# Cross attention's probabilities turned in 32x32 blocks by VectorE, and four tiles' values multiplied together on 32x32 tiles of TensorE

## Chip, cores and metric

The kernel runs on one core of one Trainium2 chip. The metric is device time in microseconds, the median of several runs. Below, PE is TensorE, PEld its weight loads, DVE is VectorE, ACT is ScalarE, POOL is GpSimd and SP is SyncE, whose queue issues nearly all DMAs.

## Reference

An encoder layer over a context of 77 tokens and a decoder layer over 2048 tokens, for two batches, in float32, with width 512, 16 heads of 32 and a feed forward of width 2048. What matters here is the decoder's cross attention, whose keys and values come from the encoder's 77 rows:

```python
memory = encoder(ctx)                                   # (2, 77, 512)
y = tgt                                                 # (2, 2048, 512)
y = y + mha(ln(y), ln(y), self weights, causal + relative bias)
y = y + mha(ln(y), memory, cross weights, relative bias)
h = ln(y)
y = y + relu(h @ ff1.T + b1) @ ff2.T + b2

def mha(xq, xkv, ...):
    q, k, v = projections of xq, xkv, xkv               # split into 16 heads of 32
    attn = softmax(q k^T / sqrt(32) + bias)
    return (attn v, heads joined) @ w_out.T + b_out
```

## The kernel before, in words

The whole schedule is written by hand: each engine executes its instructions in the order in which the program issues them. In a first part (to about 1650 us) the encoder and the decoder's self attention run. The second part does cross attention and feed forward. It is cut into 8 *blocks* of 512 tokens (2 batches of 4), and each block into four *tiles* of 128 tokens.

For each block the feed forward takes 56 *slots* (`per`). In slots 0 to 27 `first_product` (L1638) multiplies one weight tile by the block's activations, eight matmul instructions of 256 columns; the matrix products use Strassen's seven products in Winograd's form, so there are sums and differences of quarters in all places. Results go to `hT`, added by VectorE (L1651) or copied by ScalarE (L1648), and then go through ScalarE's relu (L1654). In slots 28 to 55 `second_product` (L1667) takes seven weight tiles in each four slots (2, 2, 2, 1), eight instructions of 128 columns a tile. `sums_h` (half sums L1587; others L1605, L962) prepares its left operands four slots ahead, on VectorE and GpSimd. After each four slots the sums in PSUM are mixed (L1675 to L1683) and added to `y` by GpSimd (L1687).

A float32 matmul is recorded as two instructions (two passes), a transpose as one.

`cross(x)` plans the cross attention of block x into the slots of block x - 1: each of the 56 entries of `plan` is a list of functions, run ahead of the slot's feed forward work. Only blocks 1 to 7 go through it (the first block's cross attention is `first_cross`, done within the first part with the same `attend_stages`). For each tile t of the block, with `at = 13 + 5 t`:

- slot `at`: scores. 16 matmuls (L836), one per head, of 32 partitions each, into four PSUM banks; VectorE takes the maximum (L845) and subtracts it (L846), after adding a bias (L843) for the first two tiles of a batch. The probabilities lie in `pr`, 128 queries x 16 heads x 77 keys.
- `at + 2`: exponential on ScalarE (L849).
- `at + 3`: sums (L854), reciprocals (L855) on VectorE, then GpSimd multiplies (L860).
- `at + 7`: `turned`. 16 TensorE transposes of 128x77 (L866), four to a bank, and four ScalarE copies (L867) to `pts`.
- `at + 11`: `times_v`. 16 matmuls (L874), one per head, values of 77x32 as the stationary operand and 128 queries moving, on four column strips of the array; ScalarE copies the result (L878), and for each second tile `sums_o` makes the sums S1 to S4 (L1785 to L1788).

`o_product` (L1801, result added by L1805) multiplies the output weights in slots 31 to 34 for tiles 0 and 1 and in 40 to 43 for tiles 2 and 3; `norm_stages` for the feed forward's norm (statistics L793 to L797, centring L803, transposes L811 and copies L814) starts in slots 35, 36, 44 and 45. The query projections (`q_product`, L1758) are in slots 9 to 12. Cross attention's PSUM banks are 0 to 3, taken in turn by `bank()`; the feed forward's are 4 to 7.

Weights come in tiles of 256 KB. `feed` (L1541 to L1550) issues their DMAs into a ring of 16 places in the lower half of `pp`, after each slot's products; a place is filled again as soon as PE has read it. `next_w` hands them out in order. Loads of y for a later block (`new_y`, L1361) are issued in slots 28 to 31, stores of the result (L1695) in slots 54 and 2, all from SP's queue.

Of the kernel before, what the change touches and what calls it, by code (L numbers as in the profile page):

```python
# [54 lines left out]
def tile_encoder_decoder(ctx: ExitStack, tc: tile.TileContext, ins, out):  # L55
# [103 lines left out]
    with (  # L159
# [664 lines left out]
        def attend_stages(q, kTc, v, y, biased, pr, pts, place, w_o, bi=None):  # L824


            prh = pr.rearrange("p (h k) -> p h k", k=S)
            by_r = pr.rearrange("p (g r k) -> p g r k", r=HC, k=S)
            keep = {}

            def score():
# [7 lines left out]
                for r in range(HC):  # L839
                    s = banks[r][:, : NC * S].rearrange("p (g k) -> p g k", k=S)  # L840
                    d = by_r[:, :, r, :]
                    if biased:
                        nc.vector.tensor_tensor(d, s, bi[r] if bi else d, ALU.add)  # L843
                        s = d
                    nc.vector.tensor_reduce(mx[:, :, r], s, AX.X, ALU.max)  # L845
                    nc.vector.tensor_tensor(d, s, mx[:, :, r, None].to_broadcast([P, NC, S]), ALU.subtract)  # L846

            def exp():
                nc.scalar.activation(pr, pr, AF.Exp)  # L849
# [496 lines left out]
        prs = [oflat[:, : H * S], pts_all[:, 5:8, :].rearrange("p a k -> p (a k)")[:, : H * S]]  # L1346
        kTc = pts_all[:, 4, : NC * S].rearrange("p (c k) -> p c k", k=S)
        n2_sums, o_sums, vc, qT = [high[:, (4 + k) * D : (5 + k) * D] for k in range(4)], [], [], []
# [21 lines left out]
        def last_loads():  # L1370
            t = sb.tile([P, MB], F32, name="q", tag="q", bufs=3)
            nc.sync.dma_start(t[:S, :], cv_d[:, 0, :])
            vc.append(t)
            xt_ring.append(sb.tile([P, MB], F32, name="q", tag="q", bufs=3))
# [10 lines left out]
        xt_ring, row_ca = [], []  # L1385
# [126 lines left out]
        O_SLOTS = {at + k: js for at in (31, 40) for k, js in enumerate(((0, 1), (2, 3), (4, 5), (6,)))}  # L1512
# [25 lines left out]
        w_ring = [low[:, ts(j, D)] for j in range(16)]  # L1538
        tiles, fed, used = weight_tiles(), [0], [0]

        def feed(upto):  # L1541
            while fed[0] < upto:
# [3 lines left out]
                dst = w_ring[fed[0] % len(w_ring)]  # L1546
# [5 lines left out]
        def next_w(c):  # L1552
            used[0] += 1
            assert used[0] <= fed[0]
            return w_ring[(used[0] - 1) % len(w_ring)].rearrange("p (c o) -> p c o", c=c)
# [14 lines left out]
        mixed = oflat[:, H * S : H * S + 12 * P].rearrange("p (k n) -> p k n", n=P)  # L1570
# [133 lines left out]
        def ff_slot(s):  # L1704
# [11 lines left out]
            feed(used[0] + len(w_ring))  # L1716
# [10 lines left out]
        def cross(x):  # L1727
# [4 lines left out]
            def place(tag):  # L1732
                if tag == "xr":
                    return lambda: sb.tile([P, D], F32, name=tag, tag=tag, bufs=2)
                return next_xt

            for t in range(TB):
                fs = norm_stages(
                    lambda t=t: y_of(x, t), "n2", row_ca[0], place("xt"), lambda t=t: nT2[:, :, ts(t, P)]
# [34 lines left out]

            def of_o(t, name):
                if name[0] == "S":
                    i = int(name[1]) - 1
                    return o_sums[i // 2][:, ts(i % 2, TOK)]
                r, c = int(name[0]) - 1, int(name[1]) - 1
                return held["o", t + r]["oT"][:, ts(c, TOK)]  # L1780

            def sums_o(t):
                s = {n: of_o(t, n) for n in ("S1", "S2", "S3", "S4", "11", "12", "21")}
                a21, a22 = (held["o", t + 1]["bank"][:, ts(c, TOK)] for c in range(2))
                minus(ve, s["S3"], s["11"], a21)  # L1785
                minus(ve, s["S2"], a22, s["S3"])
                ve.tensor_tensor(s["S1"], s["21"], a22, ALU.add)
                minus(gp, s["S4"], s["12"], s["S2"])  # L1788
# [20 lines left out]
            for n, js in O_SLOTS.items():  # L1809
                t = 0 if n < 36 else 2  # L1810
                plan[n].append(lambda t=t, js=js: [o_product(t, j) for j in js])
            bias_1 = None
            if m == 0:

                def next_batch():
                    nc.sync.dma_start(kTc, ckT_d[:, :, ts(b, S)])
                    nc.sync.dma_start(vc[0][:S, :], cv_d[:, b, :])
# [3 lines left out]
                spare = [y_of(x + 1, r) for r in range(HC)]  # L1821
                bias_1 = [a[:, : NC * S].rearrange("p (g k) -> p g k", k=S) for a in spare]
                plan[3].append(lambda: bias_tile(prs[0].rearrange("p (h k) -> p h k", k=S), 2, P, S, 255))
                plan[5].append(lambda: [bias_tile(a, 2, P, S, 255 - P, r, HC) for r, a in enumerate(bias_1)])
            for t in range(TB):
                at = 13 + 5 * t
# [3 lines left out]
                    lambda g, t=t: qT[g // 2][:, g % 2, ts(t, P)], kTc, vc[0][:S, :], y, biased, prs[t % 2],  # L1830
                    lambda g: pts_all[:S, g, :], place("xr"), wbt,
                    bias_1 if biased and t else None,
                )
                held["o", t] = fs[7]
                if t % 2:
                    fs = fs[:5] + (lambda t=t, f=fs[5]: [f(), sums_o(t - 1)],)

                for k, f in zip((0, 2, 3, 3, 7, 11), fs):
                    plan[at + k].append(f)
                fs = norm_stages(y, "n3", bo, place("xt"), lambda t=t: nTt[:, :, ts(t, P)])  # L1840
                at = (35, 36, 44, 45)[t]
# [152 lines left out]
```

## Time and profile before

| | |
|---|---|
| median of 3 runs | 2729.82 us (2728.53 to 2731.02) |
| span of the profiled execution | 2726.8 us |
| PE busy | 2708.1 us (99%) |
| VectorE, ScalarE, GpSimd busy | 1839.9, 1537.0, 1002.4 us |
| one block of the second part (2078 to 2215 us) | 137.0 us |

The profiled execution has its span only, from its first to its last instruction; its time as the runs count it is not listed. Busy times are unions of the instructions' durations, so a pipelined matmul counts until its end. In a group's line the columns are the line of the code, the engine, the operation, output and inputs with shapes, the count, busy time and mean ns of one, and the idle time of the engine just before them with what ended it. In a timeline's line they are start, length, engine, line, operation and count.

### The profile page before, as it was taken

Reading aid. Unit: us, or ns where it says so; the run is one execution under the profiler, and the core shown is the slowest. Engines: PE = TensorE matmul, PEld = TensorE weight load, DVE = VectorE, ACT = ScalarE, POOL = GpSimd, SP = SyncE. Lnnn points to the kernel's source line nnn. Section 1 sums busy time; section 2 is a strip of 40 time slices with the busy share of each in tenths; the row PEclk is TensorE's granted clock in tenths of the full one; section 3 lists DMA queues with packets and bytes.
Section 4 is the critical chain, followed back from the end, with each engine's and each line's share of the span. In section 5 each row is a group of like instructions: output and inputs, shape, how many; then the busy total and the mean of one; then the engine's idle time right before and its main releaser. Section 6 shows DMA issues by size and latency. Waiting matters only on the chain.

```text
span 2726.8 us, 68267 instructions
## 1 busy us (share of the span) xinstructions
PE 2708.1 (99%) x26606; PEld 2217.9 (81%) x26606; DVE 1839.9 (67%) x5445; ACT 1537.0 (56%) x2978; POOL 1002.4 (37%) x844
## 2 busy tenths in 40 slices
PE   9999999999999999999999999999999999999998
PEld 6678877777876677777777777898989898989898
DVE  4776688888885677788888783646464746464645
ACT  3554567777786547667777784444444444444431
POOL 2612235500300513322300203455556565656456
PEclk9999999999999999999999999999999999999999
DMA  8724355511213522343311206565657565656465
GB/s 242 213 92 135 126 155 164 168 50 43 67 45 89 143 76 72 111 133 98 126 50 35 79 19 220 171 214 173 213 171 239 168 216 170 218 166 219 151 224 185
DMA packets 296277, 385.10 MB, mean 141 GB/s; under 512 B 41184, under 2 KB 165648, under 8 KB 295826
## 3 DMA queue, kind: packets, MB, share of 16 engines
q1 hardware_dynamic: 295954, 380.73, 44.1%
q8 instruction: 211, 3.46, 0.5%
q14 instruction: 112, 0.92, 0.1%
HBM read 334.15 MB, written 46.47 MB: 140 GB/s over the span
## 4 chain that ended last, share of the span: by engine, by line
PE 95%; DVE 1%; ACT 1%; DMA 1%; POOL 1%; issue 1%; SPq 0%; DVEq 0%; POOLq 0%; ACTq 0%
PE psum L427 18%; PE psum L1638 14%; PE psum L1667 13%; PE psum L375 11%; PE psum L456 9%; PE psum L1134 8%; PE psum L1801 3%; PE psum L1758 3%; PE psum L1049 3%; PE psum L866 2%; PE psum L836 1%; PE psum L874 1%; PE psum L590 1%; PE psum L811 1%; PE psum L239 1%; PE psum L215 1%
## 5 line engine op out<-in xcount | busy, mean ns | idle before, releaser
L406 ACT ACTIVATE pp<-pp,nm 128x128 f32<-128x128 f32 (+15 forms) x512 | 611.8, 1200 | 28.6 <-DVE nm L401 27.8
L384 DVE TENSOR_SCALAR_CACHE_REDUCE pp<-psum 128x512 f32<-128x512 f32 (+3 forms) x1024 | 556.2, 591 | 51.3 <-PE psum L375 49.7
L434 ACT COPY pts<-psum 128x512 f32<-128x512 f32 x714 | 384.1, 594 | 312.6 <-PE psum L427 265.6
L427 PE MATMUL psum<-ident,pp 128*128 128x128 f32 x4352 | 530.4, 277 | 4.7 <-ACT nT L310 4.0
L427 PEld LDWEIGHTS psum<-ident,pp 128*128 128x128 f32 x4352 | 474.0, 141 | 55.7 <-DVE pp L384 21.4
L375 PE MATMUL psum<-kT,q 32*128 32x512 f32 (+3 forms) x2560 | 336.5, 559 | 2.5 <-DVE q L217 1.0
L456 PEld LDWEIGHTS psum<-pts,vv 128*32 128x32 f32 x8704 | 226.4, 110 | 127.4 <-DVE pp L384 55.4
L1667 PE MATMUL psum<-pp 128*128 128x128 f32 x2560 | 304.5, 276 | 1.9 <-POOL pp L962 1.6
L1667 PEld LDWEIGHTS psum<-pp 128*128 128x128 f32 x2560 | 296.3, 192 | 8.6 <-issue 2.8
L432 DVE COPY pts<-psum 128x512 f32<-128x512 f32 x374 | 245.2, 685 | 82.6 <-PE psum L427 80.3
L456 PE MATMUL psum<-pts,vv 128*32 128x128 f32 x8704 | 279.6, 276 | 0.8 <-DVE mx L391 0.3
L962 POOL TENSOR_TENSOR pp<-pp 128x512 f32<-128x512 f32 x159 | 212.8, 1356 | 111.0 <-DMA pp<-in_dec_ff_wT_dram 50.6
L1638 PE MATMUL psum<-vv,pp 128*128 128x256 f32 x1024 | 236.2, 381 | 0.0
L375 PEld LDWEIGHTS psum<-kT,q 32*128 32x128 f32 x2560 | 146.3, 183 | 107.1 <-issue 41.3
L1638 PEld LDWEIGHTS psum<-vv,pp 128*128 128x128 f32 x1024 | 190.3, 190 | 25.8 <-issue 0.5
L391 DVE CUSTOM_DVE_ANT_0 pp<-psum,bias 128x256 f32<-128x256 f32 (+1 forms) x512 | 196.0, 411 | 19.7 <-PE psum L375 19.7
L1651 DVE TENSOR_TENSOR kT<-kT,psum 128x512 f32<-128x512 f32 x96 | 65.8, 686 | 191.6 <-PE psum L1638 191.4
L1654 ACT ACTIVATE kT<-kT,vecs 128x256 f32<-128x256 f32 x192 | 86.9, 501 | 156.6 <-DVE kT L1651 155.9
L1638 PE MATMUL psum<-nT,pp 128*128 128x256 f32 x768 | 174.1, 380 | 0.5 <-DVE oT L471 0.5
L1638 PEld LDWEIGHTS psum<-nT,pp 128*128 128x128 f32 x768 | 144.2, 190 | 20.8 <-issue 1.4
L1675 ACT COPY oT<-psum 128x128 f32<-128x128 f32 x56 | 15.0, 268 | 238.9 <-PE psum L1667 238.9
L494 POOL TENSOR_TENSOR oT<-rirows,oT 128x512 f32<-128x512 f32 x30 | 38.4, 1280 | 293.6 <-DMA rirows<-rec 181.7
(272 smaller groups left out, 4110.6 us busy)
## 6 DMA issues: line engine op xcount, KB each, us to landing
pp<-w_d SPq DMA_DIRECT2D x520, 256.0 KB
pp<-in_dec_ff_wT_dram SPq DMA_DIRECT2D x112, 256.0 KB
bias<-tzg SPq DMA_DIRECT2D x128, 128.0 KB
pp<-wo_d SPq DMA_DIRECT2D x56, 256.0 KB
wqk<-in_dec_sa_in_wT_dram SPq DMA_DIRECT2D x52, 256.0 KB
wqk<-sa_q SPq DMA_DIRECT2D x84, 128.0 KB
vv<-in_enc_ff_wT_dram SPq DMA_DIRECT2D x8, 1024.0 KB
xr<-in_x_dram SPq DMA_DIRECT2D x32, 256.0 KB
```

The source lines that it names most:

```text
L375: nc.tensor.matmul(banks[r][:, : kn * P], q[rows4(r), ts(t, P)], kT[rows4(r), g, k0 * P : (k0 + kn) * P], start=True, stop=True,)
L384: nc.vector.tensor_scalar(p[:, k0 : k0 + far], s[:, :far], 1.0, None, ALU.mult, ALU.max, accum_out=st["mx"][:, r, c : c + 1],)
L391: nc.vector.tensor_tensor_reduce(p[:, k0 + far : i + 1], s[:, far:kn], near[:, 2 - (kn - far) :], 1.0, LOWEST, ALU.add, ALU.max, accum_out ...
L406: nc.scalar.activation(p, p, AF.Exp, bias=nm, accum_out=to)
L427: nc.tensor.transpose(pt[:, ts(x, P)], state[n]["p"][r][:, k], ident)
L432: nc.vector.tensor_copy(pts[:, : len(load), :], pt[:, :w])
L434: nc.scalar.copy(pts[:, : len(load), :], pt[:, :w])
L456: nc.tensor.matmul(ot[rows4(r)], vv[:, k, ts(g * HC + r, HD)], got.pop((n, k, r)), start=k == k0 and (whole or not begun), stop=k == k1 - ...
L962: engine.tensor_tensor(out, a, b, ALU.subtract)
L1134: nc.tensor.matmul(mm[:, ts(f, TOK)], left[:, c, ts(f, P)], right[:, c, :], start=c == 0, stop=c == 1,)
L1638: nc.tensor.matmul(mm[:, ts(f, TOK)], a[:, c, ts(f, P)], b[:, c, :], start=fresh and f == 0 and c == 0, stop=c == 1, skip_group_check=True,)
L1667: nc.tensor.matmul(psum[:, bank_i, ts(col, P)], lhs[:, c, :], w[:, c, :], start=fresh and k in (0, 3) and c == 0, stop=c == 3, skip_group_ ...
```

## The change

1. The probabilities of all four tiles of a block are kept (`prs`, in the lower half of `pp`, which was the weight ring), each head with 96 places of which 77 are used. VectorE turns a whole tile's probabilities, 128x1536, in 32x32 blocks in place, by one instruction (`blocks_turned`), six slots after the tile's scores. PE's transposes and ScalarE's copies of them are gone.
2. The values are loaded in three pieces of 32 keys, four times, one for each quarter of the partitions (`load_v`, 12 DMAs; the last piece is filled up with zeros). `times_v(g)` multiplies four heads for all four tiles of the block: 3 pieces x 4 quarters x 4 heads = 48 matmuls of 32x32 weights and 128 columns (4 tiles x 32 queries), where the quarter sets the row strip and the PSUM bank and the head the column strip. The four lots are in slots 32 to 35.
3. `values_out` in slot 35 reads the four banks: ScalarE copies to rows for each tile, VectorE and GpSimd make the sums for both pairs of tiles.
4. Scores start in slots 13, 17, 21 and 25, output products in 37 and 41, norms in 41, 42, 45 and 46.
5. The weight ring has ten places: four that remain in `pp` and six of `oT`; the first 22 weight tiles still use the old places.

```diff
+        def heads_of(pr):
+            return pr.rearrange("p (h k) -> p h k", h=H)[:, :, :S]
...
             def exp():
-                nc.scalar.activation(pr, pr, AF.Exp)
+                nc.scalar.activation(prh, prh, AF.Exp)
...
-        prs = [oflat[:, : H * S], pts_all[:, 5:8, :].rearrange("p a k -> p (a k)")[:, : H * S]]
+        KC = 3
+        prs = low[:, : TB * H * KC * RB].rearrange("p (a x) -> p a x", a=TB)
+        v4 = pts_all[:, :KC, :]
...
-        O_SLOTS = {at + k: js for at in (31, 40) for k, js in enumerate(((0, 1), (2, 3), (4, 5), (6,)))}
+        SCORE_AT = (13, 17, 21, 25)
+        VALUES_AT = 32
+        OUT_AT = (37, 41)
+        NORM_AT = (41, 42, 45, 46)
+        O_SLOTS = {at + k: js for at in OUT_AT for k, js in enumerate(((0, 1), (2, 3), (4, 5), (6,)))}
...
-        w_ring = [low[:, ts(j, D)] for j in range(16)]
+        w_places = [low[:, ts(j, D)] for j in (*range(16), *range(6, 12))]
+        w_ring = [low[:, ts(j, D)] for j in range(12, 16)] + [oT_all[:, j, :] for j in range(6)]
...
-        def feed(upto):
-            while fed[0] < upto:
+        def feed(upto=None):
+            while upto is None or fed[0] < upto:
+                dst, before = w_place(fed[0])
+                if before is not None and before >= used[0]:
+                    return
...
+            def load_v(batch):
+                for a in range(P // RB):
+                    for c in range(KC):
+                        n = min(RB, S - c * RB)
+                        nc.sync.dma_start(v4[a * RB : a * RB + n, c, :], cv_d[c * RB : c * RB + n, batch, :])
...
+            def blocks_turned(t):
+                nc.vector.transpose(prs[:, t], prs[:, t])
+
+            def times_v(g):
+                if g == 0:
+                    for _ in range(P // RB):
+                        bank()
+                pT = prs.rearrange("p t (h c q) -> p t h c q", h=H, c=KC)
+                for c in range(KC):
+                    for a in range(P // RB):
+                        for r in range(HC):
+                            h = g * HC + r
+                            nc.tensor.matmul(
+                                psum[rows4(r), a, ts(g, P)], v4[ts(a, RB), c, ts(h, HD)],
+                                pT[ts(a, RB), :, h, c, :], start=(c == 0), stop=(c == KC - 1),
+                            )
...
+            def values_out():
+                got = psum[:, : P // RB, :].rearrange("p a (g t q) -> p t g a q", g=NC, t=TB)
+                for t in range(TB):
+                    g0 = 2 * (t % 2)
+                    nc.scalar.copy(split(o_rows[t])[:, g0:], got[:, t, g0:])
+                for t in (0, 2):
+                    f = {n: split(of_o(t, n)) for n in ("S1", "S2", "S3", "11", "22")}
+                    a21, a22 = (got[:, t + 1, 2 * c : 2 * c + 2] for c in range(2))
+                    minus(ve, f["S3"], f["11"], a21)
+                    minus(ve, f["S2"], a22, f["S3"])
+                    ve.tensor_tensor(f["S1"], a21, f["22"], ALU.add)
+                    minus(gp, of_o(t, "S4"), of_o(t, "12"), of_o(t, "S2"))
...
+            for g in range(NC):
+                plan[VALUES_AT + g].append(lambda g=g: times_v(g))
+            plan[VALUES_AT + NC - 1].append(values_out)
             for t in range(TB):
-                at = 13 + 5 * t
+                at = SCORE_AT[t]
...
-                for k, f in zip((0, 2, 3, 3, 7, 11), fs):
+                fs = fs[:4] + (lambda t=t: blocks_turned(t),)
+                for k, f in zip((0, 2, 3, 3, 6), fs):
                     plan[at + k].append(f)
-                fs = norm_stages(y, "n3", bo, place("xt"), lambda t=t: nTt[:, :, ts(t, P)])
-                at = (35, 36, 44, 45)[t]
+                fs = norm_stages(y, "n3", bo, next_xt, lambda t=t: nTt[:, :, ts(t, P)])
+                at = NORM_AT[t]
```

80 lines of the change are left out of this document (38 added, 42 removed).

## Prediction

> **What bounds the kernel.** I read the page first, for the share of each engine and the chain that ended last.
>
> ```profile
> span 2726.8 us, 68267 instructions
> PE 2708.1 (99%) x26606; PEld 2217.9 (81%) x26606; DVE 1839.9 (67%) x5445; ACT 1537.0 (56%) x2978; POOL 1002.4 (37%) x844
> PE 95%; DVE 1%; ACT 1%; DMA 1%; POOL 1%; issue 1%; SPq 0%; DVEq 0%; POOLq 0%; ACTq 0%
> ```
>
> TensorE (PE) is the bound. The edit lies in the second part of the program, where one block's feed forward runs in 56 slots and the next block's cross attention is spread between them. The windows of one such block, and the chain of waits from 1700 to 2560 us, say how tight that part is.
>
> ```profile
> core 0: us, PE busy (x) PEld busy (x) DVE busy (x) ACT busy (x) POOL busy (x), PEclk, DMA share, GB/s
> 2078.00:2215.00 137.00, 136.98 (x1080) 124.25 (x1079) 80.15 (x157) 57.73 (x123) 78.47 (x67) 1.00 0.65 204
> by line: PE psum L1638 37.6%; PE psum L1667 31.1%; PE psum L1758 8.6%; PE psum L1801 8.4%; PE psum L866 5.4%; PE psum L836 3.3%; PE psum L874 2.9%; PE psum L811 2.6%; issue 0.0%
> ```
>
> A block takes 137.0 us, PE is busy for 136.98 of them at full clock, and every piece of the chain is a PE line. What leaves PE there leaves the time, until another engine is late. Seven blocks carry cross attention in this form (28 tiles); the first block's is done elsewhere and keeps its form.
>
> **What PE loses.** Per tile of 128 tokens, 16 transposes (L866) and 16 value products (L874, two instructions each) go.
>
> ```profile
> L866 PE MATMUL psum<-ident,oT 128*77 128x128 f32 x224 | 28.1, 274 | 0.0
> L866 PE MATMUL psum<-ident,pts 128*77 128x128 f32 x224 | 26.7, 273 | 0.0
> L874 PE MATMUL psum<-pts,q 77*32 77x128 f32 x896 | 30.3, 276 | 0.0
> 2137.40 1.99 PE L1638 MATMUL psum<-vv,pp 128*128 128x256 f32 x8
> 2139.32 1.08 PE L874 MATMUL psum<-pts,q 77*32 77x128 f32 x32
> 2140.33 1.99 PE L1638 MATMUL psum<-nT,pp 128*128 128x256 f32 x8
> 2142.16 1.91 PE L866 MATMUL psum<-ident,pts 128*77 128x128 f32 x16
> 2143.91 1.89 PE L1638 MATMUL psum<-nT,pp 128*128 128x256 f32 x8
> 2145.64 3.62 PE L1638 MATMUL psum<-vv,pp 128*128 128x256 f32 x16
> ```
>
> The transposes are busy for 54.8 us in 28 groups, 1.96 each; the timeline shows that 0.16 of a group lies over the next line (1.91 long, but the next line starts after 1.75). So 1.80 goes per tile. Eight L1638 take 2145.64 - 2143.91 = 1.73 undisturbed, 1.92 before the L874 group and 1.83 after it: entering and leaving small tiles costs 0.19 + 0.10, of which 0.10 at the first belongs to the score group ahead of it, so 0.19 in all. With the group's own 1.01 that is 1.20. Per block 4 x (1.80 + 1.20) = 12.0 us go.
>
> **What PE gains.** Four lots of 48 value products, 96 instructions each, on 32x32 tiles, in slots 32 to 35. No such tile is in the trace. A round of 128 columns takes 1.75 / 16 = 0.109. The 32 instructions of the L874 group need 8 rounds, 0.87 of its 1.01, so four column strips work abreast; the rest and the two changes of mode are 0.33. The score products (L836) show the same for four row strips, each into a bank of its own, as the lots write theirs.
>
> ```profile
> 2149.18 1.13 PE L836 MATMUL psum<-pts,bias 32*128 32x77 f32 x32
> 2150.24 2.05 PE L1667 MATMUL psum<-pp,kT 128*128 128x128 f32 x16
> 126.81 0.74 PE L645 MATMUL psum<-pp 77*32 77x77 f32 x32
> 127.48 1.33 PE L637 MATMUL psum<-ident,pp 77*77 77x77 f32 x16
> ```
>
> The two ends: sixteen abreast is 6 rounds, 0.65 + 0.33 = 0.98 a lot; four abreast is 24 rounds, 2.62 + 0.33 = 2.95. I take 0.98, because strips by columns and strips by rows are each shown four abreast and use different inputs and outputs. Four lots: 3.9 us per block. PE's own balance is -12.0 + 3.9 = -8.1 us per block, -57 us in all.
>
> The Trainium skill, "TensorE: Matmul & The Clock Gate", Part 1, gives a floor of about 25 ns from one matmul's start to the next however small it is; a lot would by it take an estimated 2.4 + 0.33 = 2.7 us and seven blocks 34 us more than now, with the wait below. The L645 group denies it in that form: 32 instructions in 0.67 us are 21 ns each.
>
> **What VectorE (DVE) gains, and who waits.** This is where most of the 57 us go back. One new instruction per tile turns 128x1536 in 32x32 blocks.
>
> ```profile
> L484 DVE STREAM_TRANSPOSE rt<-ri 128x32 f32<-128x32 f32 x30 | 6.3, 212 | 1.0
> L795 DVE TENSOR_SCALAR crs<-cmv 128x1 f32<-128x1 f32 x64 | 9.8, 153 | 2.2
> L854 DVE TENSOR_REDUCE csu<-pts 128x16 f32<-128x1232 f32 x14 | 20.0, 1432 | 23.4 <-ACT pts L849 23.4
> L855 DVE RECIPROCAL cri<-csu 128x16 f32<-128x16 f32 x32 | 8.1, 253 | 1.1
> L1587 DVE TENSOR_TENSOR pp<-kT 128x512 f32<-128x512 f32 x32 | 23.8, 766 | 0.0
> L1605 DVE TENSOR_TENSOR pp<-kT 128x512 f32<-128x512 f32 x24 | 21.2, 883 | 0.0
> L1651 DVE TENSOR_TENSOR kT<-kT,psum 128x512 f32<-128x512 f32 x96 | 65.8, 686 | 191.6 <-PE psum L1638 191.4
> L1676 DVE TENSOR_TENSOR oT<-psum,oT 128x256 f32<-128x256 f32 x56 | 23.3, 417 | 40.2 <-ACT oT L1675 40.2
> 2137.48 0.48 DVE L845 TENSOR_REDUCE cmx<-psum 128x4 f32<-128x308 f32 x1 [0.28 <-PE psum L836]
> 2141.16 0.68 DVE L1651 TENSOR_TENSOR kT<-kT,psum 128x512 f32<-128x512 f32 x1
> 2194.70 7.31 PE L1667 MATMUL psum<-pp 128*128 128x128 f32 x64
> ```
>
> Its price: L854 reads 1232 columns in 1.43, 1.16 ns a column, so 1536 are 1.78 us. The far end comes from the transpose of 32 columns: less a one-column instruction (L795) it has 59 ns for 32, 1.84 ns a column, so 0.15 + 2.83 = 3.0 us. The gap of 32 columns is too small to tell a start-up from a rate; I take 1.78 and keep 3.0 for the range. "VectorE: DVE Perf Modes" of the Trainium skill, in its part on the transpose paths, gives 311 ns for 128 bf16 columns; with the 212 above that is an estimated 1.03 ns a column and 1.76 us, though no run here shows that size.
>
> The lots need all four tiles turned, and DVE works in order. I compare both engines from the third tile's scores (slot 21) to the first lot (slot 32). Nothing of cross attention is left for PE in between but two score groups.
>
> PE: 2 scores at 1.06 + 0.19 (from 2149.18 to 2150.24, and the mode), 7 first products at 1.73, and the 7 weight tiles of slots 28 to 31 at 0.89 each (8 instructions of the 64 that ran through from 2194.70): 2.5 + 12.1 + 6.3 = 20.9 us.
>
> DVE, in its queue: 2 x 8 score reductions and subtractions at 3.7 a set (2137.48 to 2141.16), 7.4; the turns of tiles 1, 2 and 3, 5.3; sums and reciprocals of tiles 2 and 3, 3.4; four L1651 of slots 22 to 25, 2.7; two L1605, 1.8; four L1587, 3.1; one L1676, 0.4. Together 24.1, and it can't begin before the first score group is done, 1.3 later. That ends at 25.4, 4.5 us after PE stands at the lot. In the same chain the exponential of the last tile makes DVE wait a little: L854 idled for 23.4 us in 14 times before, 1.7 each, and I keep 0.7 of it, since DVE now arrives later. So PE waits 5.2 us ahead of the first lot in each block, with its own product of slot 32 and all later ones queued behind. DVE had slack here before because PE still had transposes and value products between.
>
> After the last lot (slot 35) the four banks must be read out before slot 37's first output product: a ScalarE (ACT) copy of 0.6, then six VectorE operations of 0.42 (as L1676), some 3.3 us with the handovers, while PE has 3 weight tiles, 2.7. I put 0.7 there.
>
> **What costs nothing.** ACT loses 16 copies a block (L867, rows below) and gains no more than four; it had 79 idle us in the block's window. POOL's normalisation keeps its length, and its row shows what it waits for: VectorE. The loads of values in twelve pieces come twice in the program, in slots 1 and 10, behind which the weight loads wait; a full ring covers those slots, where a tile lasts 1.73. The ring of ten instead of sixteen leaves nine tiles, 9 x 0.89 = 8.0 us, from a place's release to its next use.
>
> ```profile
> L867 ACT COPY pts<-psum 77x512 f32<-77x512 f32 x112 | 57.1, 586 | 20.4 <-PE psum L866 20.4
> L860 POOL TENSOR_TENSOR pts<-pts,cri 128x1232 f32<-128x1232 f32 x14 | 31.5, 2251 | 59.0 <-DVE cri L855 59.0
> 2193.80:2213.80 20.00, 20.00 (x178) 19.90 (x178) 10.36 (x23) 5.33 (x13) 12.48 (x12) 1.00 0.83 268
> pp<-w_d SPq DMA_DIRECT2D x520, 256.0 KB
> vv<-y SPq DMA_DIRECT2D x24, 256.0 KB
> ```
>
> At 0.83 of the DMA engines' time they moved 268 GB/s, so about 323 at most. Slots 28 to 31 will want 7 tiles and 4 loads of y, 2.9 MB or 8.9 us, in 6.3 us of PE's time; the 2.6 us of arrears lie within the 8.0, and the wait at slot 32 lets the queue catch up.
>
> **The sum.** Per block -12.0 + 3.9 + 5.2 + 0.7 = -2.2 us; seven blocks, -15 us. The span would be 2711.6. The median of the runs, 2729.8, is 3.0 above the span, and I leave that as it is: 2714.6, say 2715. Time from run to run differs by 2.5 us, so 0.2% (5.5 us) is about what a measurement can tell from no change.
>
> **Rivals.**
> - *The lots run slower, and the kernel is slower.* The place is PE in slots 32 to 35. The decisive point is 2.2 / 4 above my price: a lot of 1.5 us, 12 ns an instruction. The fastest group of the trace, L645, took 21 ns with its tail and about 17 without; if that is a limit of issue, a lot is 96 x 0.0166 + 0.33 = 1.9 and the total 2715 + 7 x 4 x 0.92 = 2741. Four abreast makes 2715 + 7 x 4 x 1.97 = 2770. For it: nothing in the trace is issued faster. Against it: L645's rounds of 77 columns (0.066) explain its pace without such a limit. Chance 0.22, with 0.04 of it within 0.2%.
> - *The turn takes 3.0 us.* Three in the stretch add 3.7 to the wait: 2715 + 7 x 3.7 = 2741. For it: the 212 ns. Against it: the other rows' rate. Chance 0.10.
> - *The ring starves PE*, because loads of y and weights collide in the shorter slots 28 to 31: 2 us a block give 2729. For it: 8.9 us of transfers in 6.3. Against it: PE waits anyway just behind. Chance 0.08, 0.05 within 0.2%.
> - *No wait at the first lot*, if VectorE keeps up: 2715 - 36 = 2679. Against it: the two sums above. Chance 0.05.
>
> **The numbers.** My forecast has 0.55, of which 0.03 is within 0.2%. Faster 0.52 + 0.05 = 0.57; same 0.03 + 0.04 + 0.05 = 0.12; slower 0.18 + 0.10 + 0.03 = 0.31. The range 2699 to 2752 leaves out the case without a wait and the slower half of the first rival, about 0.16; it covers a wait at slot 32 between 3 and 8 us and a turn between 1.78 and 3.0.
>
> **What would show it.** L866 and L874 of the seven blocks are gone from PE's groups; the new product's line has 96 instructions in about 0.8 us of each lot. The transpose of 128x1536 has a mean near 1.78. PE's waits show the new product waiting for VectorE's turn, seven times about 5 us, and little else; VectorE is busy almost throughout slots 21 to 31. A lot of over 1.5 us, a turn of over 2.3, or PE waiting for a DMA would prove me wrong.

## The result, and the profile after

The changed kernel takes 2769.25 us, the median of four runs (2766.32 to 2774.15); the kernel before took 2730.1 beside it. The ratio is 1.0148, with a 95% interval of 1.0134 to 1.0163: slower by 1.5%, where 2715 us, and so faster, was forecast. The profiled execution took 2766.32 us, its span is 2764.5, 37.7 more than before. First the page of the changed kernel, with the busy time of the engines and the shares of the chain that ended last.

```profile
PE 2685.6 (97%) x27950; PEld 2192.0 (79%) x27950; DVE 1906.8 (69%) x5473; ACT 1474.9 (53%) x2866; POOL 997.9 (36%) x845
PE 83%; DVE 10%; ACT 3%; issue 2%; POOL 1%; DMA 1%; SPq 0%; DVEq 0%; ACTq 0%; POOLq 0%
```

TensorE is busy for 22.5 us less than before, in a longer span, and VectorE's share of the chain has gone from 1% to 10%. PE executes 1344 matmul instructions more. Next the windows of one block of feed forward with its cross attention (columns as in the prediction), then four stretches around the first lot of that block.

```profile
1961.30:2103.60 142.30, 134.25 (x1274) 120.92 (x1273) 85.64 (x153) 48.89 (x108) 77.16 (x67) 0.98 0.60 181
2018.00:2024.00 6.00, 6.00 (x55) 5.85 (x53) 5.43 (x7) 3.64 (x8) 1.23 (x1) 1.00 0.74 211
2024.00:2027.00 3.00, 0.04 (x1) 0.00 (x0) 3.00 (x4) 0.00 (x0) 2.38 (x2) 1.00 0.97 354
2027.10:2033.80 6.70, 3.95 (x104) 3.39 (x105) 6.67 (x7) 0.00 (x0) 6.18 (x5) 0.50 0.35 132
2033.90:2045.00 11.10, 10.65 (x336) 8.87 (x336) 1.64 (x4) 1.00 (x3) 4.08 (x3) 1.00 0.52 145
```

The block takes 142.3 us instead of 137.0, and PE is idle for 8 of them. At 2024.0 PE stops, 3 us later its granted clock falls to 0.50 and stays there for 6.8 us, the first lot and the next products with it. In six of the seven blocks the clock record has a stretch of half clock of 6.83 us at this place, in one of 10.24. Before, there was none in the blocks. The lengthening of the seven blocks (4.3, 5.2, 5.3, 8.6, 5.1, 4.1 and 5.2 us) adds up to the whole 37.8.

The groups of the new instructions and PE's waits in the second part (engine, line, what it waited for: us in all, times, longest) say who was late.

```profile
L1815 PE MATMUL psum<-pp,pts 32*32 32x128 f32 x2688 | 47.9, 315 | 43.2 <-DVE pp L1804 42.7 <-issue 0.4
L1804 DVE STREAM_TRANSPOSE pp<-pp 128x1536 f32<-128x1536 f32 x28 | 49.5, 1769 | 0.0
PE psum L1815 <- DVE pp L1804: 42.7, 7, 7.9
PE psum L1854 <- DVE pts L1833: 9.1, 7, 1.3
PE psum L1854 <- DVE vv L1858: 3.4, 7, 0.5
```

The turn costs 1.77 us, as forecast. The first lot waits for the last turn for 6.1 us a block. The output products (L1854) wait 1.3 us for the values to leave the banks (L1833), and 0.5 for the result of an earlier output product to be added (L1858). No wait is for a DMA. The timeline of the same block shows PE, then VectorE's queue in the same stretch.

```profile
2022.99 1.06 PE L1687 MATMUL psum<-pp,kT 128*128 128x128 f32 x8
2029.85 2.17 PE L1815 MATMUL psum<-pp,pts 32*32 32x128 f32 x96 [5.81 <-DVE pp L1804]
2031.95 2.95 PE L1687 MATMUL psum<-oT,pp 128*128 128x128 f32 x16
...
2018.59 1.77 DVE L1804 STREAM_TRANSPOSE pp<-pp 128x1536 f32<-128x1536 f32 x1
2020.90 1.44 DVE L857 TENSOR_REDUCE csu<-pp 128x16 f32<-128x1232 f32 x1 [0.54 <-ACT pp L852]
2022.37 0.25 DVE L858 RECIPROCAL cri<-csu 128x16 f32<-128x16 f32 x1
2022.54 3.89 DVE L1607 TENSOR_TENSOR pp<-kT 128x512 f32<-128x512 f32 x3
2026.36 0.41 DVE L1696 TENSOR_TENSOR pts<-psum,pts 128x256 f32<-128x256 f32 x1
2026.69 1.41 DVE L1607 TENSOR_TENSOR pp<-kT 128x512 f32<-128x512 f32 x1
2028.03 1.76 DVE L1804 STREAM_TRANSPOSE pp<-pp 128x1536 f32<-128x1536 f32 x1
```

VectorE has one idle moment, 0.54 us for the exponential of the last tile; from there 8.9 us of its queue lie ahead of the end of the last turn, at 2029.8. PE has 3.2 us of work left at that moment. The two products behind the lot, 16 instructions, take 2.95 us at half clock; behind a lot at full clock they take 2.05, as the second experiment shows.

### The profile page after: what moved, and what is told of

Same layout as the page of the kernel before. It is cut to its first block, busy times and chain, and to the rows that moved or that the text cites. A ratio compares the mean times of both kernels' runs of the same rounds, so it can differ in the third digit from the quotient of the medians.

```text
span 2764.5 us, 70789 instructions
## 1 busy us (share of the span) xinstructions
PE 2685.6 (97%) x27950; PEld 2192.0 (79%) x27950; DVE 1906.8 (69%) x5473; ACT 1474.9 (53%) x2866; POOL 997.9 (36%) x845
## 4 chain that ended last, share of the span: by engine, by line
PE 83%; DVE 10%; ACT 3%; issue 2%; POOL 1%; DMA 1%; SPq 0%; DVEq 0%; ACTq 0%; POOLq 0%
PE psum L427 18%; PE psum L375 11%; PE psum L1687 10%; PE psum L1658 9%; PE psum L456 9%; PE psum L1137 8%; PE psum L1773 3%; PE psum L1854 3%; PE psum L1052 2%; PE psum L1815 2%; DVE pp L849 1%; DVE cmx L848 1%; DVE csu L857 1%; PE psum L590 1%; PE psum L811 1%
## 5 line engine op out<-in xcount | busy, mean ns | idle before, releaser
L965 POOL TENSOR_TENSOR pp<-pp 128x512 f32<-128x512 f32 x159 | 206.8, 1321 | 107.4 <-DMA pp<-in_dec_ff_wT_dram 50.9
L1687 PE MATMUL psum<-oT,pp 128*128 128x128 f32 x1544 | 193.6, 280 | 0.4 <-POOL pp L965 0.4
L1687 PEld LDWEIGHTS psum<-oT,pp 128*128 128x128 f32 x1544 | 186.3, 195 | 6.2 <-issue 3.5
L1695 ACT COPY pts<-psum 128x128 f32<-128x128 f32 x56 | 15.1, 269 | 307.9 <-PE psum L1687 307.9
L863 POOL TENSOR_TENSOR pp<-pp,cri 128x1232 f32<-128x1232 f32 x32 | 75.6, 2363 | 272.9 <-DVE cri L858 248.7
L1658 PE MATMUL psum<-vv,oT 128*128 128x256 f32 x600 | 138.2, 381 | 0.0
L1687 PE MATMUL psum<-pp 128*128 128x128 f32 x1016 | 132.4, 284 | 1.8 <-POOL pp L965 1.2
L1687 PEld LDWEIGHTS psum<-pp 128*128 128x128 f32 x1016 | 126.1, 199 | 6.8 <-issue 2.7
```

The costliest lines, as they stand in the source:

```text
L965: engine.tensor_tensor(out, a, b, ALU.subtract)
L1658: nc.tensor.matmul(mm[:, ts(f, TOK)], a[:, c, ts(f, P)], b[:, c, :], start=fresh and f == 0 and c == 0, stop=c == 1, skip_group_check=True,)
L1687: nc.tensor.matmul(psum[:, bank_i, ts(col, P)], lhs[:, c, :], w[:, c, :], start=fresh and k in (0, 3) and c == 0, stop=c == 3, skip_group_ ...
```

## The experiments

Each kernel is the changed one with the edit shown; a kernel built on an earlier experiment says so. The kernel before ran beside them at 2729 to 2730 us.

**Is it the wait, the half clock, the lots or the ring?** Four kernels test the wait, the half clock, the turn and the ring, one each; the lots follow below. The first moves the lots four slots back:

```diff
-        VALUES_AT = 32
-        OUT_AT = (37, 41)
-        NORM_AT = (41, 42, 45, 46)
+        VALUES_AT = 36
+        OUT_AT = (41, 45)
+        NORM_AT = (45, 46, 49, 50)
```

> The lots go to slots 36 to 39, the output products to 41 to 44 and 45 to 48, the last norms four slots later; nothing else changes. Theory A (TensorE's wait for VectorE's turns at the first lot, 5.8 us a block, and the half clock that follows it, about 2.5 us a block, ate the gain): the four slots give PE 6.2 us of work ahead of the lot, the wait falls to under 0.5 us, the clock stays at 1.0 through the blocks, and the time is 2769 - 7 x 8.2 = 2712 us, between 2700 and 2722. Theory B (the lots themselves, four tiles abreast, cost it): the wait goes somewhere else or the lots stay as dear, and the time stays over 2750. Theory C (the ring of ten starves TensorE): over 2760, PE waits for a DMA in the later slots.

Measured: 2752.31 us, 1.0080 (1.0065 to 1.0095). The wait at the lots is gone, but theory A is missed by 40 us: the time lies in the range of theory B, which said that the wait goes somewhere else. The lots no longer wait for the turn, and PE's waits have a new first row, which the profile cannot name ("issue"). The last two lines are PE and VectorE in one block:

```profile
PE psum L1687 <- issue: 19.5, 7, 4.6
PE psum L1854 <- DVE pts L1833: 9.2, 7, 1.4
...
2026.46 1.13 PE L1687 MATMUL psum<-oT,pp 128*128 128x128 f32 x8 [2.50 <-issue]
2022.46 3.90 DVE L1607 TENSOR_TENSOR pp<-kT 128x512 f32<-128x512 f32 x3
```

It lies ahead of the first products of slot 32 (2.5 us in this block, and 0.5 more with VectorE's half sums as the named cause). PE goes on 0.1 us after VectorE's third half sum (L1607) ends. The half sums stand at the same place in VectorE's queue as in the changed kernel, where the wait at the lot hid them. A stretch of half clock stayed in each block, 3.41 us long in six and 6.83 in one.

The second fills the wait and changes nothing else:

```diff
+                    busy = bank()
+                    for _ in range(48):
+                        nc.tensor.transpose(busy[:, :P], ident, ident)
-                    for _ in range(P // RB):
+                    for _ in range(P // RB - 1):
                         bank()
```

> The changed kernel with 48 idle 128-column transposes of the identity (about 5.2 us) on TensorE ahead of the first lot of each block, where it stood still for 5.8 us. They go to a bank that the lot overwrites. Theory A: the lot still starts when VectorE's turn is done, but the granted clock stays at 1.0, the first lot takes 1.2 us from its first to its last start instead of 1.76 and the next products 1.78 instead of 2.95; 2.5 us a block, 2769 - 18 = 2751 us, between 2745 and 2757. If the half clock has another cause than the standstill (the small tiles themselves, or the load), the clock falls as before and the time is 2769 or a few us more.

Measured: 2756.09 us, 1.0098 (1.0083 to 1.0113): 13.2 us less than the changed kernel, for work that is thrown away.

```profile
2020.14 5.40 PE L1810 MATMUL psum<-ident 128*128 128x128 f32 x48
2026.12 1.48 PE L1818 MATMUL psum<-pp,pts 32*32 32x128 f32 x96 [0.58 <-DVE pp L1804]
2027.54 2.05 PE L1687 MATMUL psum<-oT,pp 128*128 128x128 f32 x16
```

The lot still starts when VectorE is ready, and then it and the next products run at full clock (1.48 and 2.05 instead of 2.17 and 2.95). In the seven blocks the clock fell only once, in the block where PE still waited for 2.7 us. So the half clock comes from standing still, not from the small tiles, and it cost 1.9 us a block. The changed kernel's own trace agrees: the slot of the first lot is 5.4 us long on average there, 2.0 more than the 3.40 of an undisturbed slot with a lot.

The third leaves out `nc.vector.transpose(prs[:, t], prs[:, t])`.

> The changed kernel without VectorE's transposes; it leaves out the turn of the probabilities, so the lots multiply them unturned. VectorE has 3 x 1.77 = 5.3 us less to do before the first lot. Theory A: the wait falls from 5.8 to between 0.3 us (VectorE's sums) and 1.5 us (GpSimd's normalisation of the last tile, which then ends last); no half clock; 2769 - 7 x (5 + 2.5) = 2716 us, between 2708 and 2726. Theory B (the lots): over 2750. If VectorE's time before slot 32 is not what the lot waits for, the wait stays and the time is within 2760 to 2772.

Measured: 2732.28 us, 1.0016 (1.0006 to 1.0025). 37 us go, 16 fewer than expected: the lot then waits for GpSimd's normalisation (L863) instead, 1.7 us a block, and four of the seven blocks still had a stretch of half clock, where none was expected.

```profile
PE psum L1815 <- POOL pp L863: 11.7, 7, 3.4
```

The fourth is the kernel before with `range(10)` for `range(16)` in its ring. It feeds its first sixteen tiles before any is used, so that six of them are overwritten; that changes what the first block multiplies, not the time.

> The kernel before with a weight ring of ten tiles instead of sixteen, and nothing else of the change. Theories A and B: 2730 us within 3 us, PE waits for no DMA in the second part. Theory C (the ring): 2740 to 2769 us, with PE waiting for weight tiles.

Measured: 2729.17 us, 1.0001 (0.9992 to 1.0010), and no wait for a DMA in the second part. The ring of ten costs nothing there, and in the changed kernel no wait of PE is for a DMA either.

**What does a lot cost, and why?** In all kernels with the lots spread over four slots, a lot in an undisturbed slot adds 1.61 us (a slot of 3.40 instead of 1.79). This one, with the lots in slots 36 to 39, gives each product 64 columns:

```diff
-                                psum[rows4(r), a, ts(g, P)], v4[ts(a, RB), c, ts(h, HD)],
-                                pT[ts(a, RB), :, h, c, :], start=(c == 0), stop=(c == KC - 1),
+                                psum[rows4(r), a, g * P : g * P + 2 * RB], v4[ts(a, RB), c, ts(h, HD)],
+                                pT[ts(a, RB), :2, h, c, :], start=(c == 0), stop=(c == KC - 1),
```

> The kernel with the lots in slots 36 to 39, where each of a lot's 48 products runs over 64 columns instead of 128; it leaves out the values of tiles 2 and 3 in the lots. A lot adds 1.61 us to its slot with 128 columns (3.40 against 1.79). Theory I (the lot is limited by the issue of its 96 instructions, some 7 ns for the first 32 that lie ready in the queue and 12 to 17 ns for the others): with 64 columns 1.35 to 1.6 us, four lots in seven blocks save at most 7 us: 2745 to 2752. Theory R (the lot is limited by its columns: rounds of 16, 8 or 4 tiles): the rounds halve, a lot falls to 0.9 to 1.1 us: 2734 to 2740.

Measured: 2746.26 us, 1.0054 (1.0035 to 1.0073). One lot of it, and one of the kernel with 128 columns:

```profile
2034.04 1.17 PE L1815 MATMUL psum<-pp,pts 32*32 32x64 f32 x96
2035.14 2.05 PE L1687 MATMUL psum<-pp 128*128 128x128 f32 x16
```
```profile
2035.27 1.49 PE L1815 MATMUL psum<-pp,pts 32*32 32x128 f32 x96
2036.68 2.05 PE L1687 MATMUL psum<-pp 128*128 128x128 f32 x16
```

The time lies in the range of theory I; the slot with a lot is 3.08 us long, so a lot adds 1.29, between what the two theories said. From the first to the last start a lot takes 1.22 us with 128 columns and 0.95 with 64. The 0.27 saved are five rounds of 64 columns at 0.0547: the rounds are those of sixteen tiles abreast, as the prediction had them (four abreast would have saved over 1 us, eight abreast 0.60). The first lot of the changed kernel, wholly at half clock, says the same: 1.76 us, 0.54 more than at full clock, which is five rounds of 0.109 once more; eight abreast would need eleven rounds of 0.219 there, 2.4 us. What the prediction left out is the rest: 0.67 us in all three, whatever the columns and the clock. In the start records, the first 32 matmuls of a lot follow each other in 6.7 ns but for one pause, the others mostly come singly or in pairs every 17, and these spacings are the same at half clock; only the pauses between rounds grow.

Lots one after the other would save changes between large and small tiles. Two kernels issue all four in one slot: one in slot 39 with the rest as in the kernel with the later lots, and one in slot 38 with VectorE's queue as in the kernel with the late turns below. The edit is the same:

```diff
-                plan[VALUES_AT + g].append(lambda g=g: times_v(g))
-            plan[VALUES_AT + NC - 1].append(values_out)
+                plan[39].append(lambda g=g: times_v(g))
+            plan[39].append(values_out)
```

> The kernel with the lots in slots 36 to 39, but all four lots one after the other in slot 39: three pairs of changes between large and small tiles go, and three lots no longer have 32 instructions waiting in the queue. If a lot keeps the 1.22 us from its first to its last start, four cost about 5.3 us instead of 6.45, -8 us in seven blocks; if the queue's head start is lost, 5.9 us, -4 us. PE reaches slots 36 to 38 earlier, where VectorE's half sums can be late. 2740 to 2752 us.

> The order of VectorE's queue as in the kernel with the turns late, and all four lots one after the other in slot 38, so that the copies out of the banks have a slot more before the output product of slot 41. Theory O: 2728 less 4 to 8 for the lots together and less up to 7 for the banks: 2718 us, between 2708 and 2730. Theory W: over 2735.

Measured: 2779.78 us, 1.0186 (1.0170 to 1.0203), and 2752.76, 1.0081 (1.0064 to 1.0098). Both miss. Instead of 6.4 the lots took 7.4 to 10.6 us a block, in part at half clock. The timeline of the second of these kernels:

```profile
2036.72 3.02 PE L1815 MATMUL psum<-pp,pts 32*32 32x128 f32 x209
2041.64 2.81 PE L1815 MATMUL psum<-pp,pts 32*32 32x128 f32 x128 [1.90 <-issue]
2045.11 1.38 PE L1815 MATMUL psum<-pp,pts 32*32 32x128 f32 x47 [0.66 <-issue]
```

209 matmuls run through, then PE stands still, waiting for no engine; 128 more, then another hole. 128 matmuls with their weight loads are 256 instructions. In the DMA records of this kernel, blocks of 16 KB leave on the instruction queue at 2039.4 and 2042.8 us, 1 us long each, and PE goes on 1.3 us after each has landed. The DMA part of the page of the changed kernel has this queue as its second row: 221 blocks of 16.4 KB.

```profile
q1 hardware_dynamic: 296562, 381.68, 46.2%
q8 instruction: 221, 3.62, 0.6%
```

To tell a supply that runs out from a slow issue of small products, the same kernel with one of the three chunks (`for c in range(1)`):

> The kernel with all four lots together in slot 38, with the first of the three chunks of keys alone: 128 instead of 384 matmuls one after the other; it leaves out the products over keys 32 to 76. With 384 there were holes of 1.9 and 0.7 us behind the 209th and the 337th matmul, and 16 KB blocks of instructions arrived in the holes. Theory F (the stock of fetched instructions, at most 512 with the weight loads, runs out, and a block of 256 takes about 3.5 us to come): 128 matmuls with their loads are 256 instructions, all fetched ahead, there is no hole, and they take 1.6 to 1.9 us. Theory S (small products are issued at 26 ns on average however many there are): 3.3 us. The time by F: 2752 less 7 x 7 to 8 us: 2697 to 2710; by S: 2708 to 2722.

Measured: 2692.95 us, 0.9864 (0.9846 to 0.9882), 4 us below the range of theory F and 15 below that of theory S. The last line is from the DMA part of its page:

```profile
2018.60 1.90 PE L1815 MATMUL psum<-pp,pts 32*32 32x128 f32 x128
2020.43 3.84 PE L1687 MATMUL psum<-oT,pp 128*128 128x128 f32 x32
...
q8 instruction: 207, 3.39, 0.5%
```

128 matmuls take 1.8 us to the next product and start 13 ns apart on average, not 26, and no block has a hole in them. This kernel has 1792 matmuls and as many weight loads less than the changed one, 3584 instructions, and 14 blocks less on the instruction queue: 256 to a block, so this queue carries PE's instructions. The holes are its supply. With 384 matmuls in a row in slot 38, the blocks left 3.4 to 4.2 us apart while the lots ran, which is 13 to 16 ns an instruction. A slot with one lot and two weight tiles has 224 instructions for its 3.40 us, 15 ns each, within these rates, so that spread lots mostly escape (0.3 us of holes a block in the changed kernel), and lots one after the other do not.

The 0.67 us of a single lot are something else, for they come without a hole. Here 128 matmul instructions take 1.64 us from the first to the last start, and less seven rounds of 0.109 that leaves 0.87: about 7 ns for each in both. Whether the matmuls or their weight loads set it, no run separates.

**Why was VectorE later than the sum said?** The changed kernel without `nc.gpsimd.tensor_tensor(prh, prh, ri…, ALU.mult)`:

> The changed kernel (lots in slots 32 to 35) without GpSimd's normalisation of the probabilities, which it leaves out. VectorE's four half sums ahead of slot 32 took 1.37 us each, 0.78 before, with GpSimd's normalisation (2.4 us) and its own sums beside them. Theory P (the two engines hinder each other): the half sums take 0.8 to 1.1 us, the wait at the lot falls from 6.1 to about 4 us, 2769 - 7 x 2.5 = 2752 us, between 2742 and 2760. If the half sums stay at 1.3 us or more, other sums of GpSimd hinder them or it is not GpSimd, and the time stays over 2762.

Measured: 2750.4 us, 1.0074 (1.0056 to 1.0093). The half sums in the second part, before (L1587), changed, and in this kernel, and the wait at the lot in this kernel:

```profile
L1587 DVE TENSOR_TENSOR pp<-kT 128x512 f32<-128x512 f32 x24 | 18.2, 778 | 0.0
```
```profile
L1607 DVE TENSOR_TENSOR pp<-kT 128x512 f32<-128x512 f32 x24 | 31.8, 1367 | 0.0
```
```profile
L1607 DVE TENSOR_TENSOR pp<-kT 128x512 f32<-128x512 f32 x24 | 19.5, 852 | 0.0
PE psum L1815 <- DVE pp L1804: 28.9, 7, 5.9
```

The mean of 1.37 hides that one addition of the four is held up. The shortest, median and longest half sum of the whole program (ns), in the changed kernel and in this one:

```profile
L1607 DVE TENSOR_TENSOR pp<-kT x32: 627/684/2749, 1739.0 to 2716.1; 128x512 f32<-128x512 f32 x32
L1607 DVE TENSOR_TENSOR pp<-kT x32: 627/682/1420, 1735.4 to 2698.0; 128x512 f32<-128x512 f32 x32
```

In the block shown above, the four take 0.63, 2.75, 0.68 and 1.41 us, and 2.20 of the 2.75 lie beside the normalisation; without it they take 0.63, 0.68, 0.68 and 1.42. (The fourth runs beside GpSimd's own sums in both kernels.) The wait falls from 6.1 to 4.1 us a block, as these 2.1 us say.

**Is VectorE's load the bound, or the order of its queue?** With the lots in slots 36 to 39, the turns late:

```diff
-                for k, f in zip((0, 2, 3, 3, 6), fs):
+                for k, f in zip((0, 2, 3, 3, 6) if t < 2 else (0, 2, 3, 3, 11) if t == 2 else (0, 2, 6, 6, 10), fs):
```

> The kernel with the lots in slots 36 to 39, and in VectorE's queue the turn of tile 2 (slot 27) goes to slot 32, the sums and the normalisation of tile 3 from slot 28 to 31, its turn from 31 to 35, all behind the half sums that the second product of slot 32 needs. Theory O (the order in VectorE's queue makes TensorE stand in slots 31 and 32, 2.5 to 3 us a block, with a window of half clock of 3.4 us behind it): both go, about 1 us comes back at slot 36; 2752 - 7 x 3.5 = 2728 us, between 2718 and 2738. Theory W (VectorE has too much work from slot 13 to 36 in whatever order): the wait only moves to slot 36, over 2743.

Measured: 2757.15 us, 1.0105 (1.0090 to 1.0120). The wait for the half sums goes and comes back at the lot, 4.1 us a block (28.9 in all for the turn). The time lies where theory W had it, but this order put the last turn just ahead of the lot, so that it does not tell a late order from too much work. Then less work for VectorE, in slots 32 and 34, in 34 with the output products a slot later, and in the kernel before:

```diff
                     nc.vector.tensor_reduce(mx[:, :, r], s, AX.X, ALU.max)
-                    nc.vector.tensor_tensor(d, s, mx[:, :, r, None].to_broadcast([P, NC, S]), ALU.subtract)
+                    keep["s", r] = s
+                keep["nm"] = sm.tile([P, 1], F32, name="cnm", tag="cnm", bufs=3)
+                nc.vector.tensor_reduce(keep["nm"], mx.rearrange("p g r -> p (g r)"), AX.X, ALU.max, negate=True)
...
-                nc.scalar.activation(prh, prh, AF.Exp)
+                for r in range(HC):
+                    nc.scalar.activation(by_r[:, :, r, :], keep["s", r], AF.Exp, bias=keep["nm"])
```

> The changed kernel with less work for VectorE: one maximum for the sixteen heads of a token instead of one for each head, so that the exponential reads the scores from the banks with it as its bias (four ACT instructions of 308 columns), and VectorE's four subtractions a tile (0.48 us each) go for one small reduction. About 1.7 us a tile, 5.2 us ahead of the lot. Theory W (VectorE's load between the scores and slot 32 sets the wait): the wait falls from 6 us to between 0 and 1.5, with it the half clock: 2769 - 7 x 7 = 2720 us, between 2708 and 2735. Theory G (GpSimd's normalisation and the handovers of the last tile set it): the wait stays over 3 us, over 2740.

> The same with the lots in slots 34 to 37 and everything behind them two slots later. Theory W: no wait at the lot and none for the half sums of slot 32, no half clock; a block is 131.5 us of work, 2.3 us of waits at the output products and up to 1 us of holes in the lots: 134 to 135 us against 142.3, 2769 - 7 x 8 = 2713 us, between 2702 and 2722. Theory G: over 2735.

> The same with the output products one slot later still (slots 40 and 44), so that the copies of ScalarE and VectorE out of the banks are done when TensorE comes: the 1.3 and 0.5 us of waits there go, 2.3 us a block with what they delay: 132 to 133 us a block, 2713 - 16 = 2697 us, between 2688 and 2708. If another of VectorE's tasks is late in their place: 2705 to 2715.

> The kernel before with the same single maximum, and nothing of the change. TensorE was busy for 136.98 of a block's 137.0 us there, so all theories say that VectorE's relief is worth nothing in the blocks: 2729 us within 4.

Measured: in slot 32 2757.99 us, 1.0108 (1.0093 to 1.0123); in slot 34 2734.13, 1.0015 (1.0006 to 1.0025); with the later output products (slots 40 and 44, norms from 44) 2727.39, 0.9991 (0.9981 to 1.0000); the kernel before 2732.16, 1.0013 (1.0004 to 1.0022). Three of four are dearer than theory W said.

```profile
PE psum L1818 <- DVE pp L1807: 33.1, 7, 4.7
```

With 5 us less of work for VectorE the wait in slot 32 fell by 1.4 only, from 6.1 to 4.7. The relief lay ahead of the last exponential, which VectorE waits for anyway; behind it the queue of sums, half sums and turn took 8.9 us as before. Theory W in this form falls: not VectorE's sum from slot 21 to 32 sets the lot, but what lies behind the last exponential. Two slots more for it help (24 us), and so does the slot for the copies out of the banks (7 us of the 16 forecast). Last, the order for that queue, on top of the third of these kernels:

```diff
-                for k, f in zip((0, 2, 3, 3, 6), fs):
+                for k, f in zip((0, 2, 3, 3, 6) if t < 2 else (0, 2, 3, 3, 10) if t == 2 else (0, 2, 4, 4, 6), fs):
```

> The kernel with the single maximum, lots in slots 34 to 37 and output products from slots 40 and 44, and in VectorE's queue the sums of tile 3 go from slot 28 to 29 and the turn of tile 2 from slot 27 to 31, behind the half sums that the second product of slot 32 needs. It had waits of 1.4 and 0.5 us for these half sums in each block, 0.5 us more for the holes in the lots and half a window of half clock. Theory O (only the order is wrong): 1.5 to 2.5 us a block go, 2727 - 7 x 2 = 2713 us, between 2706 and 2721. Theory W (VectorE's load): the wait moves to the lot of slot 34, 2722 to 2732.

Measured: 2721.24 us (2719.12 to 2723.27), 0.9965 (0.9951 to 0.9978), 0.35% faster than the kernel before (the interval of the ratio lies below 1), and faster than the changed one. It lies just above the range of theory O and below that of theory W, so the waits have to decide. PE's waits in the second part, and the window of the shortest block:

```profile
PE psum L1818 <- issue: 10.4, 8, 2.4
PE psum L1690 <- POOL pp L968: 1.6, 2, 1.2
PE psum L1818 <- DVE pp L1807: 1.1, 7, 0.2
2213.90:2347.50 133.60, 132.86 (x1273) 119.76 (x1273) 80.44 (x141) 50.87 (x119) 78.69 (x67) 1.00 0.66 198
```

The waits for the half sums are gone, and those for the turns are down to 0.2 us a block, so it was the order of the queue. What is left are holes in the lots ("issue"). Each of the eight ends 1.3 to 1.6 us after a block of instructions has landed, as the holes above did, so they are the supply again; in these slots the second lot shares its slot with one weight tile, 208 instructions in 2.50 us, 12 ns each, faster than any block came. One hole (2.4 us) was followed by 6.8 us of half clock and made its block 138.6 us long. Whether other slots or fewer instructions avoid them in this kernel was not tried.

## Why the prediction was wrong

**The work removed: right.** The slots of a block without waits and at full clock add up to an estimated 131.4 us, from the slots of all blocks that nothing disturbed; less four lots of 1.61 that is 125.0, and 137.0 - 12.0 had been said.

**The turn: right** (1.77 for 1.78). So were the place of the wait (the last turn, ahead of the first lot, with all of PE's later work behind it) and the ring.

**The lot: the largest term that was mis-sized.** The step "sixteen abreast is 6 rounds, 0.65 + 0.33 = 0.98 a lot" had the rounds right and counted nothing for getting 96 matmuls and 96 loads to the array. A lot costs 1.61. That is over the 1.5 at which the first rival decides: 4 x 0.63 = 2.5 us a block, and the gain of 2.2 is gone. The rival's pace of 17 ns is in the start records, but not for the first 32 matmuls of a lot, which come in 6.7; hence 1.61 and not its 1.9. The argument against it, from the L645 group, rested on a group of 32 and could say nothing of the matmuls behind them. By itself this term makes 2733 us, not 2769. That the rival's other end, four abreast, had been worked out to 2770 is luck: four abreast is not what happened.

**The wait at the first lot: 6.1 for 5.2 us.** PE's side was right (20.9 us from the third scores to the lot in the block shown). On VectorE's side two errors nearly cancelled. The half sums were priced at 0.77 from a stretch in which GpSimd did not normalise beside them; the four took 5.5 us instead of 3.1, most of it in the one that was held up. The other terms came some 2 us shorter, as the durations in the rows overlap by up to 0.1 us from one instruction to the next, and the two sums priced by the row of L1605 took 1.2 for 1.8. Nor could the sum from slot 21 on tell what would help: the time without the subtractions shows that what counts begins at the last exponential.

**The clock: not in the sum at all.** A wait was charged at its own length. It also cost 1.9 us a block of half clock, by the kernel that fills it. Part 1 of "TensorE: Matmul & The Clock Gate" in the Trainium skill says it: after an idle window of about 3.4 us the clock is halved, in windows that run freely. The trace agrees on the windows, with 6.83 = 2 x 3.41 us of half clock behind a wait of 5.8, and often 3.41 behind one of 3. It does not agree that the window has to be idle: in the fourteen kernels with lots, cut into these windows from 1700 us on, every window in which PE was busy for less than 45% was followed by half clock, some of those between 45 and 63%, and of the fuller ones that ran at full clock none. The prediction read its row of 1.00 in the block's window as if the change left it so.

**The banks ahead of the output product: 1.8 for 0.7 us.** ScalarE's copies and VectorE's six sums took 4.1 us from the end of the last lot in the block shown, not 3.3 (1.3 of wait), and a second output product waited for the first one's result (0.5), which the prediction did not have.

Per block: -2.2 forecast, + 2.5 (lots) + 0.9 (wait) + 1.9 (clock) + 1.1 (banks) = +4.2. Measured are +5.4 on average; of the remaining 1.2, holes inside the lots are 0.3, and the two slots with the waits at the banks are 2.3 us longer than without, 0.5 more than the waits' rows say. The last 0.4 is not settled.

## What to carry to other kernels

Where an engine that never stood still gets a wait, charge the wait and the half clock behind it, and look for the wait behind that one before moving it: here several waits taken away showed the next in the same queue. Count instructions as well as columns: each small matmul instruction cost about 7 ns beyond its columns, and their instructions have to be fetched; spreading them among large ones hid most of what 384 in a row did not. And price an engine's step from a stretch in which its neighbours do what they will do beside it.

## What the runs showed of the hardware

- TensorE's products on 32x32 tiles run sixteen abreast: 0.27 us less for 64 columns less in five rounds, and 0.54 more at half clock. Beside the rounds, a lot's 96 matmul instructions take 0.67 us, whatever the columns and the clock.
- Its instructions come in blocks of 256, one every 3.4 to 4.2 us where it ran dry. "Runtime: NRT & Kernel Launch" of the Trainium skill, "Instruction fetch mechanics", has the blocks of 16 KiB, and says that the fetch is hidden because instructions are issued more slowly than they come; the holes of 1.90 and 0.66 us deny that for small products, and the measurement decides.
- VectorE's addition of 128x512 takes 0.63 to 0.68 us with the normalisation left out, and 2.75 where 2.20 of them lie beside GpSimd's normalisation of 128x1232; beside GpSimd's own sums it took 0.68 to 1.42.
- Waits of 5.8 to 7.9 us on TensorE were followed by two or three windows of 3.41 us at half clock, the wait's own tail among them. Shorter ones, down to 1.3 us, were followed by one to three in some blocks and by none in others.
